# Weight tiles quantised inside the feed-forward loop, fewer in the first unit, and a reordered end of the main loop in a perceiver layer

## The chip, the cores and the metric

The kernel runs on one core of one Trainium2 chip. The metric is the device time of one execution in microseconds (us); the time shown for a kernel is the median of its runs. One further execution was taken with the hardware profiler, and all durations of single instructions come from it.

## The reference

Three blocks with residuals, on x of shape 8 x 64 x 512 (512 rows in all):

```python
x = x + cross_attention(layernorm(x), ctx)   # ctx 8 x 1601 x 256; 16 heads of 128; q and k rms-normalised
x = x + self_attention(layernorm(x))         # causal over 64 rows, 16 heads of 32
x = x + ffn(layernorm(x))

def ternary_quant(w):                        # groups of 64 along a row, in bf16
    scale = clip(mean(|w|), 1e-8)            # per group
    return clip(round(w / scale), -1, 1) * scale

def ffn(x):                                  # w_gate_up 4096 x 512, w_proj 512 x 2048
    gate, up = split(x @ ternary_quant(w_gate_up).T)
    return rms_norm(silu(gate) * up) @ ternary_quant(w_proj).T
```

## The kernel before

**Stages.** The work goes in this order, with the times of the profiled execution: query projections of the cross attention, two heads at a time in `two_heads(n)`, n = 0 to 8 (0 to 126 us); the main loop (126 to 1389); the last unit's softmax and value projections, "behind the loop" (1389 to 1470); output projection and self attention (1470 to 1612); the feed-forward gate and up products, r = 0 to 15, 128 hidden columns each (to 1666.5); the down projection (to the end).

**The main loop** has 16 units u (8 batches, 2 groups of 8 heads) of 6 steps q, 256 context rows each. `step(u, q)` (L1102) makes scores of unit u and, from u = 1 on, weighs the context with the probabilities of unit u - 1 in seven products of half size (`pair_products`, L893) and four for the tail of 65 rows (`tail_products`, L918). They add up in four PSUM accumulators y0 to y3. `gather_first` (L937) and `gather` (L949) combine these into the outputs `a`; the probabilities' row sums are spread over the partitions by TensorE (`spread_sum`, L980), inverted on VectorE (`invert_sums`, L985, four parts) and multiplied in (`divide_half`, L970; `finish`, L989). In the loop every engine's order is written out by hand. For the unit before the last these steps stand behind the loop, still by hand on TensorE and VectorE. After that only TensorE's order is by hand, and a scheduler places the other engines' instructions when the program is built.

**Quantising.** The weights of the feed-forward part are quantised in 48 units of 128 x 512, numbers 0 to 31 for `w_gate_up` and 32 to 47 for `w_proj`. One unit is: a load (`load_weights`, L333, 256 KB, SyncE's queue); Abs and Sign on ScalarE (`magnitudes`, L349); group sums `tot`, scale `scl`, threshold `thr`, mask `m`, mask times sign, and a difference `sg` on VectorE (`quantise`, L360); a second difference and a product (`signed`, L379); then `put_by` (L384): a 32 x 32 transpose on VectorE and four stores of 32 KB to the scratch tensor `fw` from SyncE's queue. The feed-forward part reads `fw` back in loads of eight units, 2 MB: `load_fgu` for the first 32 units, `load_fp(0)` for units 32 to 39 and `load_fp(1)` for 40 to 47, all issued from GpSimd's queue.

Six units are quantised in the head loop (n = 2 to 7, set by `N0 = 2`), six in unit 0 of the main loop (every step), three in unit 1, two in each of units 2 to 14 (steps 0 and 4), one in unit 15, and the last six behind the loop by

```python
while n_q < NQ:
    wf = load_weights(n_q, mB[last][:, 0, 0:1])
    signed(*quantise(n_q, *magnitudes(wf)))
    put_by(n_q)
    n_q += 1
```

where a one-column copy on GpSimd (L345) holds each load back until `mB` is there.

**The feed-forward loop** (L1746): for each r, 16 matmuls make gate and up in two PSUM tiles, of which each has two buffers; ScalarE computes Silu (`gt`, three buffers), VectorE the product `hr` (two buffers), ScalarE and VectorE split it in two parts `hT`, ScalarE squares it, and GpSimd adds the square to `acc` (L1764), whose sums give the rms factor behind the first 32 products of the down projection. Both `load_fp` are issued at r = 7. Square, output and other passing tiles share ten buffers with the tag `t2`.

Of the kernel before, what the change touches and what calls it, by code (L numbers as in the profile page):

```python
# [9 lines left out]
F32 = mybir.dt.float32  # L10
# [9 lines left out]
P = 128  # L20
# [8 lines left out]
def perceiver_kernel(  # L29
# [296 lines left out]
                    krP[a - b * TAIL : e - b * TAIL, b, ts(g, HG)], kr[a - n0 : e - n0, :]  # L326
                )

    N0 = 2
    quantised = {}  # L330
    wpool = [None]

    def load_weights(u, behind=None):  # L333

        if u < 2 * NF:
            src = w_gu[ts(u, P), :]
        else:
            hb, dt = divmod(u - 2 * NF, ND)
            src = w_fproj[ts(dt, P), ts(hb, 512)]
        if len(wpool) == 1:  # L340
            wf = block("wf", 0)
        else:
            wf = fq.tile([P, 512], F32, tag="wf", name="wf", bufs=1)
        if behind is not None:
            nc.gpsimd.tensor_copy(wf[:, 0:1], behind)  # L345
        nc.sync.dma_start(wf, src)
        return wf

    def magnitudes(wf):  # L349
        n = len(wpool)  # L350
        aw = wpool[0].tile([P, 8, 64], BF, tag="aw", name="aw", bufs=n)
        nc.scalar.activation(aw.rearrange("p g k -> p (g k)"), wf, AF.Abs)
        sg = wpool[0].tile([P, 8, 64], BF, tag="sg", name="sg", bufs=n)
        nc.scalar.activation(sg.rearrange("p g k -> p (g k)"), wf, AF.Sign)
        wT = aw
        if n == 1:
            wT = wpool[0].tile([P, 8, 64], BF, tag="wT", name="wT")
        return aw, sg, wT.rearrange("p g k -> p (g k)")

    def quantise(u, aw, sg, wT):  # L360

        tot = small.tile([P, 8], F32, tag="tot", name="tot")
        nc.vector.tensor_reduce(tot, aw, AX.X, ALU.add)
        scl = small.tile([P, 8], BF, tag="scl", name="scl")
        nc.vector.tensor_scalar(scl, tot, 1.0 / 64, SCALE_MIN, ALU.mult, ALU.max)

        thr = small.tile([P, 8], F32, tag="thr", name="thr")
        nc.vector.tensor_scalar(thr, scl, 257.0 / 512, None, ALU.mult)
        m = wpool[0].tile([P, 8, 64], BF, tag="m", name="m")
        nc.vector.tensor_tensor(  # L370
            m, aw, thr.unsqueeze(2).to_broadcast([P, 8, 64]), ALU.is_gt
        )
        nc.vector.tensor_tensor(m, m, sg, ALU.mult)
        nc.vector.tensor_tensor(
            sg, aw, scl.unsqueeze(2).to_broadcast([P, 8, 64]), ALU.subtract
        )
        return u, m, aw, sg, wT

    def signed(u, m, aw, nd, wT):  # L379
        nc.vector.tensor_tensor(nd, aw, nd, ALU.subtract)  # L380
        nc.vector.tensor_tensor(m, nd, m, ALU.mult)
        quantised[u] = m, wT

    def put_by(u):  # L384
# [13 lines left out]
    with tc.tile_pool(name="qphase", bufs=1) as qp, tc.tile_pool(  # L398
# [197 lines left out]
        with tc.manual_schedule(  # L596
# [70 lines left out]
                        xns_q.append(normalise(x_sb, i + 2, qp, mvs[i + 2], rstds[i]))  # L667
                    next(roots[i], None)
            head_sums(0)
            loaded, early = [], []  # L670
            for n in range(H // 2 + 1):
                if n + 1 < H // 2:
                    head_sums(n + 1)
# [216 lines left out]
        add_to_sums(u, NJF, nc.gpsimd)  # L890
        s_sb.pop((u, NJF))

    def pair_products(u, p):  # L893

        if p == 0:
            new_y(u, 4)
        b11, b21, b22, r1, r2, r3, n4 = yA.pop((u, p))
        for k, h, i, b_, first in (
            (0, 0, 0, b11, True),
            (1, 0, 1, b21, True),  # L900
            (2, 1, 2, n4, True),
            (0, 1, 3, r1, False),
            (1, 1, 4, r2, False),
            (2, 0, 6, b22, False),
            (3, 1, 5, r3, True),
        ):
            if i == 3:
                a = yB.pop((u, p))
            elif i < 3:
                (a11, a12), (_, a22) = prob_blocks(u, p)  # L910
                a = a11, a12, a22
            product(yps[u][k][:, ts(h, W // 2)], b_, a[i], first and p == 0)
            yield
        s_pair.pop((u, p))
        for i in range(2):
            s_sb.pop((u, 2 * p + i))

    def tail_products(u):  # L918
        s = s_sb[u, NJF][:TAIL].rearrange("p (j h) s -> p j (h s)", j=2)
        for c in range(NC):  # L920
            for j in range(2):
                k, h = ((1, 0), (2, 1), (2, 0), (3, 0))[2 * c + j]
                product(
                    yps[u][k][:, ts(h, W // 2)], cxn[u, NY - 1][:TAIL, 0, ts(c, P)], s[:, j], False
                )

    def halves_of(t):
        return [t[:, ts(h, W // 2)] for h in range(2)]
# [169 lines left out]
    def weigh(k):  # L1098
        for _ in range(k):
            next(under_way, None)  # L1100

    def step(u, q):  # L1102
# [9 lines left out]
        ssq = small.tile([P, 2, HG], F32, tag="ssq2", name="ssq2")  # L1112
        probs = PROBS[u == last].get(q, ()) if u > 0 else ()
        fw_tile = None
        tern = ((q in TERN and (u, q) != (last, 4)) or u == 1 and q == 2 or u == 0) and n_q < NQ
        if tern:
            wf = load_weights(n_q)

# [96 lines left out]
            fw_tile = magnitudes(wf)  # L1215


        product_7()
        squares(ssq[:, 1], 1, c22)
        s = work.tile([P, 2, HG, S], F32, tag="s", name="s", bufs=8)  # L1220
# [17 lines left out]
            spread_max(u - 1)  # L1238
        nc.scalar.copy(quarters[:, 2], s_a[:, 1])  # L1239
        squares(ssq[:, 0], 0, c11)  # L1240
        if u == last and q == NQU - 1:
            spread_sum(last - 1)
        if new:
            under_way = pair_products(*new)
            weigh(3)
        if halves:
            signed(*halves.pop())
            put_by(n_q - 1)
        if fw_tile:
            halves.append(quantise(n_q, *fw_tile))  # L1250
            n_q += 1
# [32 lines left out]
    with tc.manual_schedule(  # L1284
        engines={mybir.EngineType.PE, mybir.EngineType.DVE}
    ):

        while later:
            later.pop(0)()
        wv_sb.append(load_wv(1))  # L1290
        if halves:
            signed(*halves.pop())
            put_by(n_q - 1)
        weigh(9)
        prob_sums(last - 1, NQU - 1)
        tail_products(last - 1)
        s_sb.pop((last - 1, NJF))
        under_way = pair_products(last - 1, NQU - 1)
        weigh(3)
        find_max(last)  # L1300
        mB[last] = spread_diag(mB[last])
        for i in range(4):
            invert_sums(last - 1, i)
        weigh(2)
        gather_first(last - 1, nc.vector)
        weigh(1)
        g_last = gather(last - 1, nc.vector)
        next(g_last)
        divide_half(last - 1, 0)
        weigh(9)  # L1310
        load_contexts(NU * NY)
        for _ in g_last:
            pass
        divide_half(last - 1, 1)
    with tc.manual_schedule(engines={mybir.EngineType.PE}):
        for h in range(HG // 2):
            values(h, "ks")
        spread_max(last)
        for h in range(HG // 2, HG):
            values(h, "ks")  # L1320
        x_sb = wkv.tile([P, NTT, D], F32, tag="w", name="x_again")
        nc.gpsimd.dma_start(x_sb, xf.rearrange("(t p) d -> p t d", p=P))
        for j in range(NJ):
            less_max(last, (j,))
            exponentials(last, (j,))
            add_to_sums(last, j, nc.vector)
        n_wo = 0
        for j in range(NJ):
            weigh_context(last, j)
            if j == NJ - 3:  # L1330
                find_sum(last)
            if j == NJ - 2:
                spread_sum(last)
                for i in range(4):
                    invert_sums(last, i)
        while n_q < NQ:
            wf = load_weights(n_q, mB[last][:, 0, 0:1])
            signed(*quantise(n_q, *magnitudes(wf)))
            put_by(n_q)
            n_q += 1  # L1340
        for h in range(H):
            load_wo(h)
        wa_qk = big.tile([P, ND, 2 * D], F32, tag="A", name="wa_qk")
        nc.gpsimd.dma_start(
            wa_qk, w_attn[:, 0 : 2 * D].rearrange("(c p) n -> p c n", p=P)
        )
        wa_vp = big.tile([P, 2, ND, D], F32, tag="A", name="wa_vp")
        nc.gpsimd.dma_start(
            wa_vp[:, 0], w_attn[:, 2 * D :].rearrange("(c p) n -> p c n", p=P)
        )  # L1350
        nc.gpsimd.dma_start(wa_vp[:, 1], w_aproj.rearrange("(c p) n -> p c n", p=P))
        finish(last)


        x1 = x_sb
        ops = {0: ps.tile([P, D], F32, tag=turn_of("s"), name="op", bufs=1)}
        project(ops[0], 0, range(HG))
        for h in range(HG, H):
            values(h, "k")
# [15 lines left out]
    def blk(shape, name, dtype=F32):  # L1375
        return blkp.tile(shape, dtype, tag="blk", name=name)

    def t2(shape, name):
        return work.tile(shape, F32, tag="t2", name=name, bufs=T2)

    ba = small.tile([P, 2 * ND], F32, tag="ba", name="ba", bufs=1)
    nc.sync.dma_start(ba, b_attn[0 : 2 * D].rearrange("(j p) -> p j", p=P))
# [187 lines left out]
    with tc.manual_schedule(engines={mybir.EngineType.PE}):  # L1570
# [165 lines left out]
        def load_fp(k):  # L1736
# [5 lines left out]
            )  # L1742
            fp_sb.append(t)

        acc = aw_.tile([P, NT], F32, tag="oT", name="acc", bufs=1)
        for r in range(NF):  # L1746
            gu = [gus.get((r, i)) for i in range(2)]
# [11 lines left out]
            if r == 0:  # L1759
                nc.scalar.activation(acc, hr, AF.Square)  # L1760
            else:
                sq = t2([P, NT], "sq")
                nc.scalar.activation(sq, hr, AF.Square)
                nc.gpsimd.tensor_tensor(acc, acc, sq, ALU.add)  # L1764
            if r == NF // 2 - 1:
                for k in range(NF // 8):
                    load_fp(k)
        for t in range(NTT):
            op = ps.tile([P, D], F32, tag="m", name="fop", bufs=2)
            y = t2([P, D], "fy")  # L1770
# [80 lines left out]
```

## Time and profile before

| quantity | value |
|---|---|
| median of 3 runs | 1703.69 us (1703.57 to 1704.33) |
| profiled execution, its own time | 1703.88 us |
| its span, first to last instruction | 1702.0 us |
| mean granted TensorE clock | 0.995 |
| busy in the span: TensorE / VectorE / ScalarE / GpSimd | 1655.0 / 1289.8 / 1159.2 / 1032.1 us |
| TensorE busy from 1389 to 1470 us | 65.98 of 81 us, granted clock 0.92 |

In the profile PE is TensorE, PEld its weight loads, DVE VectorE, ACT ScalarE, POOL GpSimd, SP SyncE, whose queue only issues DMAs here. L numbers are lines of the kernel before. A line of the timeline gives start, duration, engine, line, operation, tiles and, in brackets, the idle time ahead of it with what ended it. A line of a table by windows gives the window, its length, and for each engine the busy time with the number of instructions, then the granted clock, the DMA share and GB/s.

### The profile page before, as it was taken

The numbers are of one execution on the slowest core, as the hardware profiler recorded it, in microseconds if no ns is written. First come the engines' busy times: TensorE is split into PE (matmuls) and PEld (weight loads), VectorE is DVE, ScalarE is ACT, GpSimd is POOL, SyncE is SP. The second block draws the span as 40 slices with busy tenths as digits, with TensorE's granted clock in tenths as the row PEclk, the third lists the DMA queues.
The fourth block names the chain that finished last, engine by engine and source line by source line (L and its number), as shares of the span: only waits on it lengthen the run. The fifth ranks groups of instructions, "written<-read, shape, count | busy, mean of one in ns | idle before, by whom it ended". The sixth has DMA issues, their size and how long they took to land.

```text
span 1702.0 us, 22178 instructions
## 1 busy us (share of the span) xinstructions
PE 1655.0 (97%) x6068; PEld 1060.6 (62%) x6068; DVE 1289.8 (76%) x1941; ACT 1159.2 (68%) x4511; POOL 1032.1 (61%) x1244
## 2 busy tenths in 40 slices
PE   9999899999999999999999999999999989899998
PEld 5655456666666666666666666666666553366787
DVE  5777988888888887888888888888788866545641
ACT  5768787878777777878787778777787743123441
POOL 3212257778787879787787878786978854100040
PEclk9999999999999999999999999999999999999999
DMA  7113221211212111211121221111212026600330
GB/s 228 13 15 64 46 53 43 44 42 38 45 40 44 35 42 43 47 43 35 44 45 41 43 41 38 44 36 47 49 29 55 22 82 230 148 1 1 100 99 25
DMA packets 254244, 92.74 MB, mean 54 GB/s; under 512 B 208400, under 2 KB 234792, under 8 KB 254120
## 3 DMA queue, kind: packets, MB, share of 16 engines
q1 hardware_dynamic: 244762, 68.78, 18.2%
q0 software_dynamic: 8928, 22.02, 4.3%
q8 instruction: 48, 0.79, 0.2%
q14 instruction: 76, 0.62, 0.1%
q10 hardware_dynamic: 430, 0.53, 0.1%
HBM read 77.62 MB, written 7.34 MB: 50 GB/s over the span
## 4 chain that ended last, share of the span: by engine, by line
PE 69%; DVE 12%; POOL 8%; ACT 5%; issue 3%; DMA 2%; SPq 0%; DVEq 0%; POOLq 0%; ACTq 0%
PE p_u L750 15%; PE y L750 12%; PE p L750 10%; PE s_a L750 10%; PE gu L1662 4%; PE op L1061 3%; PE fop L1780 2%; PE s L750 2%; PE mm_qk L1457 2%; DVE s L724 2%; ACT c L754 1%; DVE mx L740 1%; ACT p_u L754 1%; PE kp L302 1%; PE vp L1046 1%
## 5 line engine op out<-in xcount | busy, mean ns | idle before, releaser
L754 ACT ACTIVATE c<-c 128x128 f32<-128x128 f32 x1152 | 341.7, 302 | 104.7 <-DVE c L1185 68.6
L754 ACT ACTIVATION_READ_ACCUMULATOR c<-c 128x1 f32 x1152 | 220.7, 192 | 0.0
L750 PE MATMUL p_u<-wk,cxT 128*128 128x512 f32 x384 | 196.3, 593 | 1.1 <-ACT p_u L754 1.1
L724 DVE TENSOR_TENSOR s<-s,ssq 128x1024 f32<-128x1024 f32 x96 | 135.4, 1410 | 52.9 <-ACT ssq L105 52.9
L750 PE MATMUL y<-s,cxn 128*128 128x256 f32 x540 | 145.9, 379 | 0.0
L740 DVE TENSOR_TENSOR mx<-mx,s 128x512 f32<-128x512 f32 x160 | 134.3, 839 | 5.5
L750 PEld LDWEIGHTS s_a<-aT,cxS 128*128 128x128 f32 x384 | 72.8, 190 | 93.8 <-issue 78.0
L813 DVE TENSOR_TENSOR s<-s,mB 128x1024 f32<-128x1024 f32 (+1 forms) x102 | 126.7, 1255 | 2.1 <-ACT mB L791 2.1
L754 ACT ACTIVATE p_u<-p_u 128x128 f32<-128x128 f32 x384 | 100.4, 262 | 27.8 <-PE p_u L750 18.7
L878 POOL TENSOR_TENSOR yT<-s 128x256 f32<-128x256 f32 x76 | 73.7, 970 | 69.3 <-PE y L750 67.5
L750 PE MATMUL s_a<-aT,cxS 128*128 128x256 f32 x384 | 114.4, 380 | 1.3 <-ACT s L1239 1.3
L817 ACT ACTIVATE s<-s,zero_t 128x1024 f32<-128x1024 f32 (+1 forms) x102 | 112.0, 1099 | 4.8 <-DVE s L813 4.7
L750 PE MATMUL s_a<-aT,cxT 128*128 128x256 f32 x384 | 114.7, 380 | 0.5 <-ACT half L1171 0.5
L750 PEld LDWEIGHTS y<-s,cxn 128*128 128x128 f32 x540 | 102.7, 190 | 14.3
L750 PE MATMUL p_u<-wkS,cxT 128*128 128x512 f32 x192 | 102.4, 615 | 9.1 <-DVE c L1185 8.5
L750 PEld LDWEIGHTS s_a<-aT,cxT 128*128 128x128 f32 x384 | 73.1, 191 | 51.9 <-issue 41.2
L750 PE MATMUL p_u<-wkS,cxS 128*128 128x512 f32 x192 | 99.7, 601 | 2.4 <-POOL cxS L230 1.4
L1154 ACT COPY p<-p 128x512 f32<-128x512 f32 x96 | 56.1, 584 | 64.9 <-PE p L750 63.1
L750 PE MATMUL p<-wkS,cxS 128*128 128x512 f32 x192 | 98.8, 596 | 1.4 <-POOL cxS L228 1.4
L750 PE MATMUL p<-wk,cxS 128*128 128x512 f32 x192 | 98.3, 594 | 0.6 <-ACT p L1154 0.6
L750 PE MATMUL p<-wk,cxT 128*128 128x512 f32 x192 | 98.2, 593 | 0.5 <-DVE st L712 0.5
L1185 DVE TENSOR_TENSOR c<-p_u,p 128x512 f32<-128x512 f32 x96 | 63.7, 664 | 41.2 <-PE p_u L750 41.2
(276 smaller groups left out, 4321.3 us busy)
## 6 DMA issues: line engine op xcount, KB each, us to landing
cxn<-in_ctx_dram SPq DMA_DIRECT2D x96, 256.0 KB
cxB<-in_ctx_dram SPq DMA_DIRECT2D x192, 64.0 KB
wf<-in_L_ffn_w_gate_up_dram SPq DMA_DIRECT2D x32, 256.0 KB
fgu<-fw POOLq DMA_DIRECT2D x4, 2048.0 KB, 8.2
fw<-aw SPq DMA_DIRECT2D x168, 32.0 KB
wq<-in_L_xattn_Wq_dram SPq DMA_DIRECT2D x4, 1024.0 KB
wf<-in_L_ffn_w_proj_dram SPq DMA_DIRECT2D x16, 256.0 KB
wo<-in_L_xattn_Wo_dram POOLq DMA_DIRECT2D x16, 256.0 KB, 5.4
```

Of the source, the lines that this page charges most:

```text
L724: nc.vector.tensor_tensor(flat, flat, kr.unsqueeze(2).to_broadcast([P, 2 * HG, S]), ALU.mult)
L740: nc.vector.tensor_tensor(mx[u][:r], mx[u][:r], s[:r], ALU.max)
L750: nc.tensor.matmul(out_, a, w, start=start, stop=True, skip_group_check=not start)
L754: nc.scalar.activation(k[:, ts(h, HD)], k[:, ts(h, HD)], AF.Square, accum_out=ssq[:, 4 * half + h : 4 * half + h + 1],)
L813: nc.vector.tensor_tensor(t, t, m.to_broadcast([r, len(js), W]), ALU.subtract)
L817: nc.scalar.activation(t, t, AF.Exp, bias=zero_t[: t.shape[0]], scale=1.0)
L878: eng.tensor_tensor(s1, a21, a22, ALU.add)
L1061: nc.tensor.matmul(op, o_sb[h][:, ts(t, P)], wo_sb[h], start=(h == 0), stop=(h == H - 1),)
L1154: nc.scalar.copy(p5, p_5)
L1185: nc.vector.tensor_tensor(c22, p_u, p5, ALU.add)
L1457: nc.tensor.matmul(mm[:, j, :], wa_qk[:, c, ts(ND * i + j0 + j, P)], xT_a[:, c, cols], start=(c == 0), stop=(c == ND - 1),)
L1662: nc.tensor.matmul(gu[:, cols], fgu_sb[rr // 8][:, rr % 8, c, :], xs_[n_][c][:, cols], start=(c == 0 and n_ == 0), stop=(c == ND - 1 and n ...
```

## The change

Eight units (40 to 47, all of `load_fp(1)`) are quantised in the feed-forward loop, at r in `LATE`; the loop behind the main loop is gone. The head loop takes seven units (from n = 1), unit 0 three instead of six. In the feed-forward loop three of a unit's five elementwise operations on 128 x 512 go to GpSimd, the tiles come from the shared `t2` buffers, the load is held behind `gt` of its r by a one-column copy on GpSimd, and `load_fp(1)` is issued after the last unit. Separately, for the unit before the last, the row sums are spread ahead of `product_7` of the loop's last step and inverted in that step, the products run in an order that completes y0 and y1 first, and `gather_first`, the first part of `gather` and `divide_half(.., 0)` come ahead of `find_max` and of the remaining products.

```diff
-    N0 = 2
+    N0 = 1
...
-    def quantise(u, aw, sg, wT):
+    def quantise(u, aw, sg, wT, m=None, eng=nc.vector):
...
-        nc.vector.tensor_tensor(m, m, sg, ALU.mult)
+        eng.tensor_tensor(m, m, sg, ALU.mult)
...
-    def signed(u, m, aw, nd, wT):
-        nc.vector.tensor_tensor(nd, aw, nd, ALU.subtract)
-        nc.vector.tensor_tensor(m, nd, m, ALU.mult)
+    def signed(u, m, aw, nd, wT, eng=nc.vector):
+        eng.tensor_tensor(nd, aw, nd, ALU.subtract)
+        eng.tensor_tensor(m, nd, m, ALU.mult)
...
-            loaded, early = [], []
+            loaded, early = [load_weights(0)], []
...
-        tern = ((q in TERN and (u, q) != (last, 4)) or u == 1 and q == 2 or u == 0) and n_q < NQ
+        tern = ((q in TERN and (u, q) != (last, 4)) or u < 2 and q == 2) and n_q < NQ
...
+        if u == last and q == NQU - 1:
+            spread_sum(last - 1)
         product_7()
...
-        if u == last and q == NQU - 1:
-            spread_sum(last - 1)
...
             put_by(n_q - 1)
+        if u == last and q == NQU - 1:
+            for i in range(4):
+                invert_sums(last - 1, i)
...
         prob_sums(last - 1, NQU - 1)
-        tail_products(last - 1)
-        s_sb.pop((last - 1, NJF))
-        under_way = pair_products(last - 1, NQU - 1)
-        weigh(3)
-        find_max(last)
-        mB[last] = spread_diag(mB[last])
-        for i in range(4):
-            invert_sums(last - 1, i)
+        under_way = pair_products(last - 1, NQU - 1, (0, 1, 3, 4, 6, 2, 5))
+        weigh(2)
+        tail_products(last - 1, (0,))
         weigh(2)
         gather_first(last - 1, nc.vector)
+        tail_products(last - 1, (2,))
         weigh(1)
         g_last = gather(last - 1, nc.vector)
         next(g_last)
         divide_half(last - 1, 0)
+        find_max(last)
+        mB[last] = spread_diag(mB[last])
+        tail_products(last - 1, (1, 3))
+        s_sb.pop((last - 1, NJF))
         weigh(9)
...
-        while n_q < NQ:
-            wf = load_weights(n_q, mB[last][:, 0, 0:1])
-            signed(*quantise(n_q, *magnitudes(wf)))
-            put_by(n_q)
-            n_q += 1
...
+        LATE = (1, 3, 5, 7, 9, 11, 12, 13)
...
+            if r in LATE:
+                wf = t2([P, 512], "wf")
+                nc.gpsimd.tensor_copy(wf[:, 0:1], gt[:, 0:1])
+                load_weights(n_q, wf)
+                both = t2([P, 2, 8, 64], "aw", BF)
+                m = t2([P, 8, 64], "m", BF)
+                tern = quantise(
+                    n_q, *magnitudes(wf, (both[:, 0], both[:, 1])), m, nc.gpsimd
+                )
+                signed(*tern, nc.gpsimd)
+                put_by(n_q)
+                n_q += 1
             if r == NF // 2 - 1:
-                for k in range(NF // 8):
-                    load_fp(k)
+                load_fp(0)
+            if n_q == NQ and len(fp_sb) == 1:
+                load_fp(1)
```

More of the change, by code (lines that the diff above doesn't have):

```diff
@@ L327, in tail_roots, with load_weights @@
                 )
-    N0 = 2
+    N0 = 1
     quantised = {}
     wpool = [None]
-    def load_weights(u, behind=None):
+    def load_weights(u, wf=None):
         if u < 2 * NF:
@@ L339, in load_weights, with magnitudes @@
             src = w_fproj[ts(dt, P), ts(hb, 512)]
-        if len(wpool) == 1:
+        if wf is None and len(wpool) == 1:
             wf = block("wf", 0)
-        else:
+        elif wf is None:
             wf = fq.tile([P, 512], F32, tag="wf", name="wf", bufs=1)
-        if behind is not None:
-            nc.gpsimd.tensor_copy(wf[:, 0:1], behind)
         nc.sync.dma_start(wf, src)
         return wf
-    def magnitudes(wf):
+    def magnitudes(wf, rooms=None):
         n = len(wpool)
-        aw = wpool[0].tile([P, 8, 64], BF, tag="aw", name="aw", bufs=n)
+        aw, sg = rooms or [
+            wpool[0].tile([P, 8, 64], BF, tag=n_, name=n_, bufs=n) for n_ in ("aw", "sg")
+        ]
         nc.scalar.activation(aw.rearrange("p g k -> p (g k)"), wf, AF.Abs)
-        sg = wpool[0].tile([P, 8, 64], BF, tag="sg", name="sg", bufs=n)
         nc.scalar.activation(sg.rearrange("p g k -> p (g k)"), wf, AF.Sign)
@@ L368, in quantise @@
         nc.vector.tensor_scalar(thr, scl, 257.0 / 512, None, ALU.mult)
-        m = wpool[0].tile([P, 8, 64], BF, tag="m", name="m")
+        if m is None:
+            m = wpool[0].tile([P, 8, 64], BF, tag="m", name="m")
         nc.vector.tensor_tensor(
@@ L891, in last_sums, with pair_products @@
         s_sb.pop((u, NJF))
-    def pair_products(u, p):
+    def pair_products(u, p, order=(0, 1, 2, 3, 4, 6, 5)):
         if p == 0:
@@ L897, in pair_products @@
         b11, b21, b22, r1, r2, r3, n4 = yA.pop((u, p))
[L898 to L909, printed above, removed]
+        places = (
+            (0, 0, b11, True),
+            (1, 0, b21, True),
+            (2, 1, n4, True),
+            (0, 1, r1, False),
+            (1, 1, r2, False),
+            (3, 1, r3, True),
+            (2, 0, b22, False),
+        )
+        for i in order:
+            k, h, b_, first = places[i]
+            if i >= 3:
+                a = yB[u, p][i]
+            else:
                 (a11, a12), (_, a22) = prob_blocks(u, p)
-                a = a11, a12, a22
-            product(yps[u][k][:, ts(h, W // 2)], b_, a[i], first and p == 0)
+                a = (a11, a12, a22)[i]
+            product(yps[u][k][:, ts(h, W // 2)], b_, a, first and p == 0)
             yield
+        yB.pop((u, p))
         s_pair.pop((u, p))
@@ L916, in pair_products, with tail_products @@
             s_sb.pop((u, 2 * p + i))
-    def tail_products(u):
+    def tail_products(u, which=(0, 1, 2, 3)):
         s = s_sb[u, NJF][:TAIL].rearrange("p (j h) s -> p j (h s)", j=2)
[L920 to L925, printed above, removed]
+        for i in which:
+            c, j = divmod(i, 2)
+            k, h = ((1, 0), (2, 1), (2, 0), (3, 0))[i]
+            product(
+                yps[u][k][:, ts(h, W // 2)], cxn[u, NY - 1][:TAIL, 0, ts(c, P)], s[:, j], False
+            )
     def halves_of(t):
@@ L1376, in blk, with t2 @@
         return blkp.tile(shape, dtype, tag="blk", name=name)
-    def t2(shape, name):
-        return work.tile(shape, F32, tag="t2", name=name, bufs=T2)
+    def t2(shape, name, dtype=F32):
+        return work.tile(shape, dtype, tag="t2", name=name, bufs=T2)
     ba = small.tile([P, 2 * ND], F32, tag="ba", name="ba", bufs=1)
@@ L1743, in load_fp @@
             fp_sb.append(t)
+        LATE = (1, 3, 5, 7, 9, 11, 12, 13)
+        assert n_q + len(LATE) == NQ and n_q >= 2 * NF + 8
         acc = aw_.tile([P, NT], F32, tag="oT", name="acc", bufs=1)
@@ L1764, in perceiver_kernel @@
                 nc.gpsimd.tensor_tensor(acc, acc, sq, ALU.add)
+            if r in LATE:
[6 more added lines that the diff above has]
+                    n_q, *magnitudes(wf, (both[:, 0], both[:, 1])), m, nc.gpsimd
+                )
+                signed(*tern, nc.gpsimd)
+                put_by(n_q)
+                n_q += 1
             if r == NF // 2 - 1:
-                for k in range(NF // 8):
-                    load_fp(k)
+                load_fp(0)
+            if n_q == NQ and len(fp_sb) == 1:
+                load_fp(1)
         for t in range(NTT):
```

## Prediction

> **What bounds the kernel now.** I read the page's totals first: TensorE is busy for 97% of the span, so only its idle stretches and what follows them can be won.
>
> ```profile
> PE 1655.0 (97%) x6068; PEld 1060.6 (62%) x6068; DVE 1289.8 (76%) x1941; ACT 1159.2 (68%) x4511; POOL 1032.1 (61%) x1244
> ...
> PEclk9999999999999999999999999999999999999999
> ```
>
> Second, TensorE's timeline behind the main loop, where the brackets are its idle time.
>
> ```profile
> 1396.59 9.54 PE L1046 MATMUL vp<-a,wv 128*128 128x512 f32 x16 [5.45 <-issue]
> 1406.20 7.03 PE L1046 MATMUL vp<-a,wv 128*128 128x512 f32 x16
> ...
> 1424.82 10.54 PE L841 MATMUL y<-s,cxn 128*128 128x512 f32 x24 [1.29 <-DMA cxn<-in_ctx_dram]
> ...
> 1451.88 6.04 PE L1046 MATMUL vp<-a,wv 128*128 128x512 f32 x8 [7.47 <-DVE a L993]
> ```
>
> Two holes, 5.45 and 7.47 us. The 16 matmuls behind the first take 9.54 us, the next 16 take 7.03: in the table by windows the granted clock is 0.50 from 1397 to 1400 and again from 1452 to 1456, so each hole costs some 2.5 us more. Third, what filled the holes:
>
> ```profile
> 1391.05 3.38 DVE L987 RECIPROCAL rB<-rB 128x128 f32<-128x128 f32 x4
> ...
> 1445.64 0.63 ACT L352 ACTIVATE aw<-wf 128x512 bf16<-128x512 f32 x1 [10.88 <-DMA fw<-aw]
> 1446.18 0.57 ACT L983 COPY rB<-bp 128x512 f32<-128x512 f32 x1
> ```
>
> In the first hole VectorE inverts the sums, then gathers; in the second the copy that the inversion needs stands on ScalarE behind a quantising step that waited 10.88 us for stores. Fourth, unit 0 by step (columns: PE, PEld, DVE, ACT, POOL busy):
>
> ```profile
> 163.00:176.30 13.30, 13.12 (x40) 7.12 (x39) 11.30 (x20) 10.62 (x47) 2.92 (x5) 1.00 0.30 50
> 176.30:189.20 12.90, 10.89 (x32) 5.31 (x31) 11.84 (x22) 10.28 (x48) 1.88 (x5) 1.00 0.31 54
> 189.20:201.50 12.30, 10.96 (x33) 5.67 (x32) 11.44 (x20) 8.32 (x38) 3.20 (x4) 1.00 0.22 38
> 201.50:213.00 11.50, 9.02 (x28) 4.30 (x28) 10.94 (x18) 9.49 (x46) 2.41 (x5) 1.00 0.20 37
> 213.00:226.00 13.00, 11.71 (x39) 6.64 (x38) 11.71 (x22) 11.16 (x53) 4.87 (x8) 1.00 0.37 64
> ```
>
> VectorE is dense and TensorE idle for 0.18 + 2.01 + 1.34 + 2.48 + 1.29 = 7.3 us. Last, the feed-forward part and the rows that price what moves there:
>
> ```profile
> 1666.53 7.56 PE L1780 MATMUL fop<-fp,hT 128*128 128x512 f32 x32
> ...
> L1764 POOL TENSOR_TENSOR acc<-acc,sq x15: 1287/1296/1732, 1619.7 to 1668.8; 128x512 f32<-128x512 f32 x15
> L881 POOL TENSOR_TENSOR s<-s x90: 721/728/1182, 223.6 to 1384.6; 128x256 f32<-128x256 f32 x90
> L381 DVE TENSOR_TENSOR m<-sg,m x48: 424/560/837, 56.8 to 1470.4; 128x512 bf16<-128x512 bf16 x48
> DMA to landing us min/median/max: 8.5/10.1/11.7
> ```
>
> TensorE has no gap there, 3.68 us per r (16 x 0.23). The last row is `load_fp`.
>
> **Gains, part by part.** *End of the loop.* The inversion moves into VectorE's wait of 3.19 us ahead of L724 in the last step, so it costs 0.2 us there. Behind the loop POOL's last pair sum still ends at 1388.15; maxima (to 1388.9), gather and half a division (2.4 us) then let the first `vp` start near 1391.5, when TensorE has just finished the remaining products. The hole of 5.45 shrinks by 5.1 and its half clock goes (9.54 - 6.98 = 2.6), less 1.2 us, since the copy of the first `vp` out of PSUM now queues behind the second half of the gather on VectorE: -6.4. *Behind it.* Without quantising, spread sums at 1435.8 give copy 0.6, inversion 3.4, `finish` 1.3: ready by 1441.3, while `op` matmuls cover TensorE until 1444.4. The hole of 7.47 goes, with its slow clock (6.04 - 3.49 = 2.6) and two gaps of 0.29 and 0.38: -10.7. The 1.29 us wait for `cxn` I leave: its load shares the queues with the weights whose loads GpSimd no longer holds back (0 to +3). *Unit 0.* A unit costs VectorE 4.4 us (0.67 + 0.19 + 0.17 + 0.69 + 0.42 + 0.69 in one step, 0.41 + 0.42 + 0.71 in the next). Two fewer in the dense stretch take 8.7 of its 46 busy us; ScalarE is next with 50 of 63 from 163 to 226. Of 7.3 us I take 5.5 (3 to 7.3). *Head.* n = 1 now has a unit: from 10.37 us (spacing of L534) to the 11.85 of n = 2, +1.5; and its load leaves SyncE's queue behind eleven small stores at 36.7, lands 3.05 later (as issue 1408.03 to Abs 1411.08 shows), while ScalarE reaches Abs at 37.3: +2.4 in front of the copies that TensorE needs. Head +3.9 (1.5 to 5). Sum: -6.4 - 10.7 - 5.5 + 3.9 = -18.7 (-24 to -11).
>
> **The price in the feed-forward loop.** The order in which the changed program's instructions stand on each queue decides. On VectorE the transpose of unit k stands ahead of the group sums of unit k + 1, and waits for POOL's last product of unit k; behind it wait the next `lo` and `hr`, hence the PSUM tiles and TensorE. So units do not overlap: one round runs VectorE, POOL, VectorE. On SyncE the load of k + 2 stands behind the four stores of k; on ScalarE Abs, waiting for that load, stands ahead of a Silu. On POOL a round holds product, `acc`, difference, product. The three bf16 operations on POOL are in no trace. By elements they are `acc`, 1.30 us; by bytes L881, 0.73. I take 1.30, since rows of POOL follow the element count (0.73 for 256, 1.30 for 512), and nothing shows that a narrower type is faster there.
>
> One round: `tot`, `scl`, `thr`, `m` 0.67 + 0.19 + 0.17 + 0.69, POOL 4 x 1.30 (the 0.69 of `sg` lies under `acc`), transpose 0.71, one `hr` 0.69, hand-offs 0.5: 8.8 us. TensorE makes two r in 7.4, and r = 11, 12, 13 have a unit each, so the backlog only grows. Start: Silu of r = 1 ends at 1617.5, copy 0.4, load 3.05, Abs 0.6, hand-offs: 1622.0. Eight rounds end at 1692.4; going through the queues item by item, the second and third rounds take 11 us (loads that wait for SyncE, two `acc`), which makes the last transpose end at 1697.9. Four stores of 0.62, the last landing 1.6 after its issue: 1702.0. `load_fp(1)`, alone, 8.5: **1710.6**. TensorE's loop also stretches by 10 us, but ends at 1676, does the half that `load_fp(0)` feeds, and then waits for some 30 us. Before, it read the first tile of `load_fp(1)` at 1666.53 + 3.68 = 1670.2. So the end moves by 40.4, plus 2.6 for the half clock after so long a hole: +43.0. With 0.73 per operation the load lands at 1697.9 (+30.3); with 1.7, if VectorE's work in between slows POOL as L826 (1.27, at most 2.25) was slowed, at 1719.8 (+52.2).
>
> Here a rule speaks against the change. VectorE needs 0.42 us for these bf16 products at their best, so POOL's 1.30 would be three times that. The Trainium skill, GPSIMD Engine Reference, section 8, calls VectorE structurally about twice as fast for elementwise work. By that ratio an operation would be an estimated 0.84 us, the load would land near 1700 and the sum be some 10 us lower. No run shown here decides between them.
>
> Sum: -18.7 + 43.0 = +24.3, span 1726.3; the profiled execution lies 1.9 above its span and 0.2 above the median: **1728**.
>
> **Rivals.** *Slow POOL.* At 2.0 us per operation `load_fp(1)` lands at 1726.7: +40, 1744. For it: VectorE is busy between POOL's steps. Against: `acc`, beside the same VectorE work, shows 1.30. *The front gains fail.* A late `cxn` or POOL's pair sums keep the first hole: 8 us back, 1736. *Faster: no backlog.* If units overlap and only the last one's own chain counts, Silu of r = 13 at 1658.2 gives copy and load 3.6, Abs 0.6, VectorE 1.8, POOL 3.9, `sg` and transpose 1.4, stores 4.1, load 8.5, hand-offs 0.6: 1682.7, so +12.5 + 2.6 - 18.7 = -3.6, 1700; with 0.73 on POOL 1698. It wins once the last transpose ends before 1673.5. Against: only two loads are ahead at any time, and the order on VectorE. *Nothing moves:* excluded, as all 48 units and their queues are in the built program.
>
> **How the numbers follow.** Main case 0.62, 1712 (0.73 us per POOL operation and the largest front gains) to 1740 (1.7 us and the middle ones); slow POOL 0.16; failed front gains 0.10; no backlog 0.12, of which 0.10 falls under -0.2% (3.4 us, about what the runs can tell from no change). Range 1706 to 1746: it leaves out the case without backlog and the upper part of slow POOL.
>
> **What would show it.** Right: idle PE behind the first 16 `fop` matmuls, ended by the load `fp`, 20 to 45 us long, then a clock near 0.5; `fw` stores at the end of the trace after 1675; the holes ahead of `vp` gone; POOL's bf16 rows near 1.3. Wrong: `load_fp(1)` landing less than 16 us after TensorE reaches it, or gaps left behind the main loop.

## The result, and the profile after

The changed kernel takes 1728.45 us (median of 4 runs, 1728.17 to 1729.88), the kernel before 1703.63 us beside it: a ratio of 1.0148, 95% interval 1.013 to 1.0165, or 25 us longer. Its profiled execution, the longest of the four, took 1729.88 us with a span of 1728.1 us, 26.1 us more than before.

From here on, L numbers are lines of the kernel whose trace is shown. First the totals of the page of after and the clock in forty slices (43 us each):

```profile
PE 1656.6 (96%) x6068; PEld 1063.6 (62%) x6068; DVE 1287.4 (74%) x1917; ACT 1160.2 (67%) x4511; POOL 1055.3 (61%) x1270
...
PEclk9999999999999999999999999999999999999978
```

TensorE's work is the same; the idle time lies in the last two slices. Its timeline in after, first at the end of the main loop (the two holes ahead of `vp` were there), then in the down projection:

```profile
1391.33 7.05 PE L1049 MATMUL vp<-a,wv 128*128 128x512 f32 x16
...
1437.01 13.90 PE L1049 MATMUL vp<-a,wv 128*128 128x512 f32 x32
...
1660.68 4.12 PE L1796 MATMUL fop<-fp,hT 128*128 128x512 f32 x16
1694.69 5.82 PE L1796 MATMUL fop<-fp,hT 128*128 128x512 f32 x16 [29.89 <-DMA fp<-fw]
```

Both holes are gone and the `vp` matmuls run at 7.05 us for 16. The price is above all one hole of 29.89 us, ended by the load `fp`; the 16 matmuls behind it take 5.82 us, the first 3.3 us of them at a granted clock of 0.50. GpSimd's and VectorE's own timelines show what the load waited for: the last transpose, four stores, then the issue:

```profile
1680.57 0.71 DVE L387 STREAM_TRANSPOSE aw<-m 128x512 bf16<-128x512 bf16 x1 [2.49 <-POOL m L381]
...
1686.41 0.93 POOL L1740 DMA_DIRECT2D fp<-fw  x1 [5.88 <-DMA fw<-aw]
```

The eight transposes start at 1612.9, 1623.5, 1634.8, 1645.0, 1655.5, 1664.3, 1672.5 and 1680.6: rounds (from one transpose to the next) of 8.1 to 11.3 us, one after the other.

Where the time went, by the same instruction in both traces (before to after):

| place | shift against before |
|---|---|
| first copy `p1` of the main loop (127.06 to 133.59) | +6.5 |
| unit 1, same matmul (295.39 to 296.01) | +0.6 |
| unit 14 (1295.84 to 1296.22) | +0.4 |
| last step (1369.77 to 1368.67) | -1.1 |
| first `vp` behind the loop (1396.59 to 1391.33) | -5.3 |
| r = 3 of the feed-forward loop (1618.68 to 1600.25) | -18.4 |
| end of the span | +26.1 |

So in these two traces the head cost 6.5 us, unit 0 gave back 5.9, and the front as a whole gained 18.4; the feed-forward part cost 44.5. Of these, 12.6 are TensorE's loop, stretched by the rounds (the first `fop` comes at 1660.68 instead of 1666.53, although the front gained 18.4), 29.9 are the hole, and the remaining 2.0 are the slow clock behind it.

### The profile page after: what moved, and what is told of

It reads as the page before. It is cut to its first block, busy times and chain, and to the rows that moved or that the text cites. A ratio compares the mean times of both kernels' runs of the same rounds, so it can differ in the third digit from the quotient of the medians.

```text
span 1728.1 us, 22175 instructions
## 1 busy us (share of the span) xinstructions
PE 1656.6 (96%) x6068; PEld 1063.6 (62%) x6068; DVE 1287.4 (74%) x1917; ACT 1160.2 (67%) x4511; POOL 1055.3 (61%) x1270
## 4 chain that ended last, share of the span: by engine, by line
PE 68%; DVE 12%; POOL 9%; ACT 4%; issue 3%; DMA 2%; SPq 0%; DVEq 0%; POOLq 0%; ACTq 0%
PE p_u L750 15%; PE y L750 12%; PE p L750 10%; PE s_a L750 10%; PE op L1064 3%; PE kp L302 2%; PE s L750 2%; PE mm_qk L1458 2%; PE fop L1796 2%; PE vp L1049 2%; DVE s L724 2%; ACT c L754 1%; DVE mx L740 1%; ACT p_u L754 1%; POOL den L883 1%
```

## The experiments

Chips differ by one or two us, so each run is judged by its ratio to the kernel before, timed beside it; 0.001 is 1.7 us. Against the kernel as changed (1.0148), differences of ratios are used; by the intervals of the two ratios, such a difference is uncertain by some 4 us.

**The front alone.** LATE is empty, and `load_fp(1)` reads units 32 to 39.

```diff
-        LATE = (1, 3, 5, 7, 9, 11, 12, 13)
+        LATE = ()
...
-            u = 2 * NF + 8 * k
+            u = 2 * NF
```

> The changed kernel with units 40 to 47 left out: they are not quantised at all, and the second load of the down projection reads units 32 to 39 again (so its output means nothing). Theory A (the whole price is the late second load, the front part gains what its trace shows, TensorE 18.5 us earlier at the first gate and up products): 1685 us. Rival B (part of the price lies elsewhere, for example in the shared buffers or in load and store traffic that the front part moved): over 1690 us. Rival C (the front part gains less than 10 us by itself): 1694 us or more.

Measured: 1683.54 us, ratio 0.9888 (0.9873 to 0.9904): -19.1 us against before. The front is worth what the trace says, and the units in the feed-forward part cost 0.026 or 44.3 us. Theory A holds; B and C fall.

**The reordered end alone**, with head, unit 0 and six units behind the loop as before.

> The kernel before with the reordered end of the main loop alone (sums spread and inverted in the last step, half the accumulators gathered first); the head, unit 0 and the six units behind the loop as before. Theory A (the prediction's step): the first hole goes with its half clock, -6.4 us, 1697 us. Rival B (GpSimd's last pair sum or the copies hold the first values back): -2 us or less, 1702 us. Rival C (what is gained is given back at the second hole, since the six units behind the loop end when they ended): 1702 to 1704 us, with the second hole wider than 7.5 us.

Measured: 1697.40 us, ratio 0.9966 (0.9953 to 0.9978): -5.8 us. TensorE's timeline of this run:

```profile
1391.14 7.05 PE L1049 MATMUL vp<-a,wv 128*128 128x512 f32 x16
...
1443.68 5.89 PE L1049 MATMUL vp<-a,wv 128*128 128x512 f32 x8 [7.19 <-DVE a L996]
```

The first hole is gone; the second is as long as it was (7.19 us), only earlier. Theory A.

**The load of unit 0 early in the head.**

```diff
             load_wq(3)
+            loaded, early = [load_weights(0)], []
...
-            loaded, early = [load_weights(0)], []
```

> The changed kernel with the load of unit 0 issued ahead of the small stores in the head (before the query projections, behind the last weight load) instead of after them. Theory A (in the head, ScalarE's wait of 2.77 us for this load opened a hole of 3.93 us on TensorE, and the half clock behind it cost about as much as the prediction's other term): the hole and the slow clock go, 4 to 5 us: 1723.5 us. Rival (the prediction's own figure of 2.4 us is all there is to it): 1726 us. Rival (the load takes bandwidth from the first weights, which TensorE waits for): 1728 us or more.

Measured: 1725.08 us, ratio 1.0135 (1.0122 to 1.0149): 2.2 us earlier than the changed kernel, between the figures of theory A and the first rival, and the intervals overlap. The traces say more. TensorE in after, ScalarE in after, then the copy `p1` in before, after and this run:

```profile
41.19 2.05 PE L490 MATMUL q_u<-xS,wqS 128*128 128x256 f32 x4 [3.93 <-ACT qp L532]
```

```profile
39.63 0.63 ACT L352 ACTIVATE aw<-wf 128x512 bf16<-128x512 f32 x1 [2.77 <-DMA wf<-in_L_ffn_w_gate_up_dram]
```

```profile
127.06 0.59 ACT L1129 COPY p<-p_u 128x512 f32<-128x512 f32 x1 [2.91 <-PE p_u L750]
```

```profile
133.59 0.59 ACT L1132 COPY p<-p_u 128x512 f32<-128x512 f32 x1 [2.91 <-PE p_u L750]
```

```profile
129.15 0.59 ACT L1132 COPY p<-p_u 128x512 f32<-128x512 f32 x1 [2.91 <-PE p_u L750]
```

The hole shrinks to 1.06 us, and the granted clock is 1.00 from 41 to 45 us where after had 0.50; the head costs 2.1 us instead of 6.5. So 4.4 us of the head were the late load with its half clock in these two profiled executions. But after is the extreme: nine other runs of this document have the same head, and in their traces the hole is 1.67 to 3.63 us and `p1` comes at 129.44 to 133.36, 2.4 to 6.3 us later than before, 5.0 in the median. What the late load costs thus differs from trace to trace, which fits the 2.2 us that show over all runs.

**GpSimd's operations on VectorE.** `m, nc.gpsimd` becomes `m` and `signed(*tern, nc.gpsimd)` becomes `signed(*tern)`.

> The changed kernel with the three operations of the late units on VectorE instead of GpSimd. Theory A (the rounds go from VectorE to GpSimd and back, each waiting for the other): a unit keeps VectorE 4.4 us and the round has no hand-off and no acc in it; with hr and the low part of two r VectorE needs 7.2 us per two r, where TensorE needs 7.4. Only r = 11 to 13 with a unit each fall behind: last transpose near 1657, load landed near 1670, TensorE waits 10 to 20 us: 1705 us (1698 to 1712). Rival (loads and stores through SyncE's queue set the rounds of 8 to 11 us): 1722 us or more.

Measured: 1720.77 us, ratio 1.0098 (1.0082 to 1.0113): 8.5 us earlier, 9 us above the range of theory A and at the rival's edge. Two things were wrong in the expectation. VectorE was nearly never idle in a round and still needed 8 us, as some of its operations were stretched (a difference to 1.67 us, a low part `hT` to 1.79). And the scheduler put eight stores in a row ahead of two loads. SyncE's queue in this run, and ScalarE's wait for the load:

```profile
1618.25 10.56 SPq L390 DMA_DIRECT2D fw<-aw  x8
1628.98 2.07 SPq L344 DMA_DIRECT2D wf<-in_L_ffn_w_proj_dram  x2
```

```profile
1633.33 0.63 ACT L352 ACTIVATE aw<-wf 128x512 bf16<-128x512 f32 x1 [3.42 <-DMA wf<-in_L_ffn_w_proj_dram]
```

One round took 15.9 us by it. GpSimd's hand-offs are not the only link.

**Loads from GpSimd's queue.** `load_weights` issues the late loads with `nc.gpsimd.dma_start`.

> The changed kernel with the loads of the eight late units issued from GpSimd's queue, right behind the one-column copy, so that none stands behind the four stores of a unit before it on SyncE's queue. Theory A (each round goes from VectorE to GpSimd and back, and the load behind the stores is a part of it): ScalarE's Abs waited 2.30, 1.78, 2.09, 1.58, 1.35 and 2.21 us for a load in the trace of after, 11.3 us in all; GpSimd pays up to 0.9 us for each issue: 4 to 11 us earlier, 1717 to 1724 us. Rival (the loads lie beside GpSimd's part of the round and cost nothing): 1728 us or more, since only GpSimd's issues are added.

Measured: 1729.71 us, ratio 1.0162 (1.0148 to 1.0176): 2.4 us later, which the intervals do not tell from no change. The rival's number, but not its reason: Abs still waited (3.91, 0.91, 3.73, 0.83, 3.94 and 0.79 us, 14.1 in all where after had 11.3), since the loads now stand behind a difference of the unit before or a sum `acc` on GpSimd's queue. The load was moved from one queue to another and not out of the round, so this run decides nothing about the load's share.

**Parts of the round taken out.** Next the load was left out (one tile for all units), GpSimd's work halved, and both at once.

```diff
-                wf = t2([P, 512], "wf")
+                if r == LATE[0]:
+                    wf = t2([P, 512], "wf")
+                    load_weights(n_q, wf)
                 nc.gpsimd.tensor_copy(wf[:, 0:1], gt[:, 0:1])
-                load_weights(n_q, wf)
```

```diff
-        eng.tensor_tensor(m, m, sg, ALU.mult)
+        eng.tensor_tensor(m[:, :4], m[:, :4], sg[:, :4], ALU.mult)
```

> The changed kernel in which all eight late units use the one tile that the first of them loaded (the other seven loads are left out; the one-column copy that holds a unit back stays). Theory A (the load is one more link of the ring): ScalarE's waits for it, 11.3 us in all, go: 1716 us. Rival (the load runs beside GpSimd's products and the store's issue; without it Abs would wait for the buffers instead): 1724 us or more.

> The changed kernel with GpSimd's three operations of a late unit cut to half of their columns (four of eight groups; the other half is left out). Theory A (a round is a ring VectorE, GpSimd, VectorE, in which GpSimd's time counts in full): the rows go from 1.15 to an estimated 0.6 us, 1.6 us less in each of eight rounds: 13 us earlier than the changed kernel, 1714 us. Rival (the rounds wait for loads that stand behind stores on SyncE's queue, or for VectorE's own queue, and what GpSimd saves becomes waiting): 4 us earlier at most, 1723 us or more.

> Both of the two cuts at once: GpSimd's three operations on half of their columns, and one loaded tile for all eight late units (half of the products and seven loads are left out). Each alone gave 8.5 and 3.9 us. Theory A (links of one ring): the two add, 12.4 us earlier than the changed kernel, 1715 us. Theory B (GpSimd's products and the next load are two branches of a round side by side, and each hides a part of the other): more than the sum, since neither hides the other any more: 17 us or more, 1710 us or less. Theory C (VectorE's own queue is the floor: 1.7 us of sums and mask, 0.7 to 1.8 for the difference, 0.7 for the transpose and 2.8 for hr and the low parts of two r, 6 to 7 us, beside 7.4 of TensorE for two r): no round under 7 us, so little more than one of the two alone, 1718 us.

| left out | ratio (95%) | against the changed kernel | last transpose starts |
|---|---|---|---|
| seven loads | 1.0125 (1.0110 to 1.0141) | -3.9 us | 1674.4 |
| half of GpSimd's columns | 1.0098 (1.0083 to 1.0113) | -8.5 us | 1668.9 |
| both | 1.0064 (1.0050 to 1.0077) | -14.3 us | 1664.5 |

Without the loads Abs waits for none (its longest wait is 0.62 us), and yet 3.9 of the expected 11 us show: the number is the rival's, its reason is not. One round grew to 13.9 us instead. GpSimd's and VectorE's operations stand in another order there, and a low part `hT` on VectorE, ahead of the transpose, took 4.26 us beside three operations of GpSimd in a row:

```profile
1625.48 4.26 DVE L140 TENSOR_TENSOR hT<-hr,hT 128x512 fp32r<-128x512 f32 x1 [0.69 <-ACT hT L139]
```

Halving GpSimd's columns took its operations to 0.67 to 1.06 us, 11.1 us less over the 24 of them, and gave 8.5; Abs still waited 12.3 us for loads. Together the two gave 14.3 us where the sum is 12.4. This agrees with theory A (a ring to which GpSimd and the load each add). Theory C does not fit, as three rounds took 6.6 us, under its floor of 7; B's 17 us are not excluded by the intervals. Even then the rounds were 6.6 to 11.8 us and TensorE waited 19.6 us for the load: that much of the price is left with VectorE's links, the other half of GpSimd's columns, and the stores and the load at the end; how it divides was not tried.

**The second load in halves.**

```diff
+            if n_q == NQ - 4 and len(fp_sb) == 1:
+                load_fp_half(0)
+            if r == LATE[-1]:
+                load_fp_half(1)
```

> The changed kernel with the second load of the down projection issued as two halves of 1 MB: units 40 to 43 as soon as they are stored, 44 to 47 at the end. Theory A (TensorE's 29.9 us wait is ended by the last load alone, 8.2 us from its issue for 2 MB): a half lands some 4 us sooner and the 16 matmuls of each quarter go ahead: 1724 us. Rival (the landing is set by the stores or the queue, not by the size): 1728 us.

Measured: 1722.65 us, ratio 1.0123 (1.0109 to 1.0137): 4.3 us earlier, the number of theory A. Issue to TensorE's start took 5.5 us (1684.65 to 1690.18) where the whole load took 8.3 (1686.41 to 1694.69). So 2.8 us are the smaller load; the other 1.7 by which TensorE started earlier are an earlier issue, as the last transpose came 1.5 us sooner in this trace.

**Other places for the eight units.** First in the main loop, then behind it.

```diff
+ or 2 <= u < 10 and q == 3
```

> The changed kernel with units 40 to 47 quantised in the main loop, in step q = 3 of units u = 2 to 9, instead of the feed-forward loop. Theory A: nothing is late in the feed-forward part, and what is paid is VectorE's time in the loop. VectorE is busy 10.15 of 12.2 us in such a step and 8.55 of 12.3 in the next; a unit adds 2.8 and 1.5 us, so it overruns the first step by 0.8 us: 8 x 0.8 = 6.4 us, 1691 us (1685 with no cost, 1700 if each unit costs as much as one of the three in unit 0 that went, 5.9 / 3 = 2 us). Rival (the feed-forward part stays long for another reason): over 1720 us.

Measured: 1704.27 us, ratio 1.0011 (1.0002 to 1.0020), 20.9 us more than without the units, 2.6 each and not 0.8. TensorE's timeline in step 4 of such a unit, which now has two units' work:

```profile
423.94 1.12 PE L750 MATMUL p_u<-wk,cxT 128*128 128x512 f32 x2 [1.73 <-ACT p_u L754]
```

The wait is for ScalarE's squares of `p_u`, an engine that the expectation had not counted. It shows in every second of the eight units; the other four have a wait of 1.14 us for the same squares and one of 0.92 for VectorE. Together these are 15 of the 20.9 us, 11.5 of them for ScalarE; what makes up the rest stays open.

```diff
+        while n_q < NQ:
+            wf = fq.tile([P, 512], F32, tag="wf", name="wf", bufs=1)
+            nc.gpsimd.tensor_copy(wf[:, 0:1], held[:, 0:1])  # held: inverted sums of the last unit
...
     xs.close()
```

> The changed kernel with the eight late units quantised again behind the main loop, on VectorE, but each load held until the last sums are inverted and the units written behind the last value projections, not ahead of the copy that the inversion needs; nothing in the feed-forward loop. From 1430 to 1490 us VectorE is busy 10.8 of 60 us and ScalarE 4.6 there. Theory A (the second hole of before came from where the units stood, not from their work; nothing else is late): 1683.5 us of the kernel without these units plus 0 to 6 us for copies that now stand behind a unit: 1686 us. Rival (the units cost TensorE what they cost before, 10.7 us and more, since there are eight of them instead of six): 1698 us.

Measured: 1702.65 us, ratio 1.0001 (0.9993 to 1.0010). The expectation was wrong by 16 us; the rival's 1698 was nearer. TensorE and VectorE in this run:

```profile
1492.02 1.97 PE L1445 MATMUL tp_ln<-ident,xn 128*128 128x128 f32 x8 [13.39 <-DVE xn L131]
```

```profile
1470.27 0.69 DVE L362 TENSOR_REDUCE tot<-aw 128x8 f32<-128x512 bf16 x1 [8.85 <-ACT aw L352]
```

The four units done by 1459 us cost one hole of 1.88; the other four waited for their loads (Abs 7.53 us in one case), and the next stage's normalised rows `xn` stood behind them on VectorE.

**Four and four.** This points to a mixture: four units behind the loop, four at r = 0 to 3, and the load of unit 0 early.

```diff
+        while n_q < NQ - 4:
...
+        LATE = (0, 1, 2, 3)
```

> Four late units (40 to 43) behind the loop as in the run with all eight there, where the first four were done by 1459 us at the price of one hole of 1.9 us, and four (44 to 47) in the feed-forward loop at r = 0 to 3; the load of unit 0 early. Theory A (what costs is the number of rounds in a row after r = 1: four of some 10 us end near 1643, stores by 1648, the load lands near 1656, and TensorE, stretched by some 5 us, gets there at about the same time): 1683.5 of the kernel without the units, -3 for the head, +2 behind the loop, +5 in the feed-forward loop: 1688 us (1684 to 1696). Rival (the hole ahead of the second half of the down projection stays, since the rounds are paced by r and the load by its own 8 us): over 1700 us.

Measured: 1692.22 us, ratio 0.9934 (0.9921 to 0.9946): faster than both kernels, 11 us under the kernel before. TensorE's three longest waits behind the loop in this run:

```profile
1437.51 10.72 PE L1049 MATMUL vp<-a,wv 128*128 128x512 f32 x24 [2.26 <-DVE o_h L1060]
...
1617.01 0.50 PE L1671 MATMUL gu<-xT_f,fgu 128*128 128x512 f32 x1 [2.78 <-DVE hr L1768]
1624.27 0.50 PE L1671 MATMUL gu<-xT_f,fgu 128*128 128x512 f32 x1 [1.73 <-DVE hr L1768]
```

The hole in the down projection is gone. With the transposes at 1605.6, 1613.4, 1621.2 and 1633.7 the load is issued at 1639.7, and 8.5 us later it is there before TensorE needs it. Theory A, 4 us above its figure and inside its range. The early load of unit 0 is part of this gain; alone it gave the changed kernel 2.2 us.

## Why the prediction was right, step by step

The forecast was 1728 us in 1706 to 1746; measured 1728.45. The mechanism and the order of the steps were right: one late load behind rounds that do not overlap. That the median agrees to half a us is luck: terms were off by up to 2.6 us, the head (+2.6), the price (+1.5) and the clock near 1340 (-1.5) above all; they left 1.8 us in the span (26.1 against 24.3), and the profiled execution is 1.4 us longer than the median.

- **Sum of the front: -18.7; measured -18.4 in the trace, -19.1 by the run without the late units.** *End of the loop*, -6.4: -5.8 alone. *Behind it*, -10.7: from the first `vp` (-5.3) to r = 3 (-18.4) lie 13.1 us, of which 2.5 are the slow clock of the first 16 (9.54 to 7.05) that the prediction counted with the end: 10.6. The wait for `cxn` stayed, 1.81 instead of 1.29.
- **Unit 0: -5.5; measured -5.9.**
- **Head: +3.9; measured +6.5 in this trace, 5.0 in the median of nine others. This term was mis-sized**: its range was 1.5 to 5. ScalarE's wait was right (2.77 for 2.4), but in front of TensorE it became 3.93 us, and no half clock was put behind it, though the prediction had one behind each of the other holes: 0.50 from 41 to 45 us. The Trainium skill, TensorE: Matmul & The Clock Gate, Part 1, names idle gaps over some 3.4 us, judged in a free-running window, as what halves the clock. The 3.93 us here agree; but shorter holes of this case halved it too (last section), and there the measurement decides.
- **Not foreseen: -1.5 us near 1340,** where nothing was changed. Both traces have the same hole there, and only before lost its clock; this is chance, not a gain of the change:

```profile
1339.99 2.04 PE L750 MATMUL p_u<-wkS,cxT 128*128 128x512 f32 x2 [2.06 <-DVE c L1185]
```

```profile
1340.40 1.12 PE L750 MATMUL p_u<-wkS,cxT 128*128 128x512 f32 x2 [2.07 <-DVE c L1188]
```

- **Price in the feed-forward loop: +43.0; measured 44.5 in the trace and 44.3 by the runs.** TensorE started on the late load at 1694.69, in the time scale of before 1713.1, against 1710.6 predicted for the landing. TensorE waited 29.9 us ("some 30"), and its loop stretched by 12.6 instead of 10. The 3.05 us put down for a load were read from an Abs that came straight behind a copy, where they are only an upper bound; in after the six loads that Abs waited for took 2.97 to 5.87 us from their issue to Abs.
- **The rounds**, 8.8 us with two of 11: measured 8.1 to 11.3, four of them above 10; the mean from the first transpose to the last is (1680.57 - 1612.94) / 7 = 9.7. Two `acc` stand in each of these four, where the prediction had them in two rounds only. (Its two rounds of 11 us move the last transpose from 1692.4 to 1696.8; the other 1.1 us up to its 1697.9 are in no sum that it shows.) GpSimd's operations were 1.15 us undisturbed instead of 1.30; six of the 24 took 1.48 to 1.54, so that the mean, 1.25, came near the forecast partly by luck. VectorE's difference, put at 0.69 and "under `acc`", took 1.75 in six of eight units. GpSimd's two products (L373, L381) and VectorE's difference (L374) in after, with duration min/median/max in ns, first and last start; of L374 the first row is the main loop and head, the second the late units:

```profile
L373 POOL TENSOR_TENSOR m<-m,aw x8: 1149/1160/1488, 1606.0 to 1675.2; 128x512 bf16<-128x512 bf16 x8
L381 POOL TENSOR_TENSOR m<-aw,m x8: 1148/1154/1168, 1611.8 to 1679.4; 128x512 bf16<-128x512 bf16 x8
```

```profile
L374 DVE TENSOR_TENSOR sg<-aw,scl x40: 691/693/1110, 43.7 to 1316.0; 128x512 bf16<-128x512 bf16 x40
L374 DVE TENSOR_TENSOR aw<-aw,scl x8: 689/1752/1765, 1607.5 to 1676.3; 128x512 bf16<-128x512 bf16 x8
```

- **The rule weighed in the prediction** (VectorE about twice as fast) would have given 0.84 us per operation; the rows show 1.15 against 0.42, a factor of 2.7. The element count was the better guide: 1.15 lies nearer to 1.30 than to 0.73, and half the columns, 128x256 in bf16, took 0.67 us, near the 0.73 of 128x256 in f32.
- **Rivals.** Slow POOL: none of the 24 bf16 operations took over 1.6 us, where the rival had 2.0. Front gains fail: both holes are gone. No backlog: the transposes follow one another without overlap, and only with four units (the mixture) does the end come in time. What a cheaper GpSimd operation is worth was put about right: from 1.30 to 0.73 us the prediction's sum fell by 12.7 us, which is some 10 us for the 0.46 us per operation by which the run with halved columns was cheaper; it gave 8.5, within its uncertainty.

## What to carry to other kernels

Work that is moved into another loop to fill an engine's idle time is paid by the length of its chain, not by its busy time: count the hand-offs on every in-order queue, the DMA queue's too, and multiply by the units in a row before the consumer. A few such units may be free where eight are not: four and four in two places, with the load of unit 0 early, gave 0.9934, eight in any one place 1.000 to 1.015. And every hole of more than 3 us that a forecast adds on TensorE is given its half clock as well; for one of 1.8 to 3 us it came in about half of the cases in these traces.

## What was not expected of the hardware

VectorE's difference and GpSimd's sum `acc` exclude each other, as the timelines of after show side by side, first VectorE, then GpSimd:

```profile
1607.50 1.76 DVE L374 TENSOR_TENSOR aw<-aw,scl 128x512 bf16<-128x512 bf16 x1 [1.07 <-POOL m L373]
```

```profile
1607.42 1.28 POOL L1767 TENSOR_TENSOR acc<-acc,sq 128x512 f32<-128x512 f32 x1
```

The difference begins 0.08 us behind `acc` and ends 0.56 behind its end, as it would if it waited for `acc` and then took most of its own 0.69. It does so in six of the eight late units (1.73 to 1.76 us); in the other two, at 1631.56 and 1668.92, GpSimd is idle and it takes 0.69. The 4.26 us of `hT` in the run without loads are the same: it ended 0.60 us behind the third of GpSimd's operations. The Trainium skill, SBUF — State Buffer, section "SBUF: two separate sides", says that a VectorE operation with two SBUF inputs and a GpSimd operation that reads SBUF take a port pair in turn, each for a whole instruction; these numbers agree. `hr`, whose first input is in PSUM, kept its time beside `acc` (0.68 at 1609.18).

A hole of 2.06 us halved TensorE's clock in one trace and one of 2.07 did not in the other (granted clock 0.50 and 1.00 in the 2.4 us from 1341). All fourteen traces of this case have this hole, at 2.06 or 2.07 us; six lost their clock behind it and eight did not. Over all of TensorE's holes of 1.4 us and more behind its first matmuls in these traces, none up to 1.81 us was followed by a slow clock, 18 of 38 between 1.82 and 3.03 us were, and every one of 3.25 us or more was; once, in the run with GpSimd's operations on VectorE, a hole of 1.20 us was too. What decides in between no run here shows; a hole of about 2 us is thus priced between nothing and 1.7 us of slow clock: from 1339.99 and from 1340.40 the same matmuls up to `y` take 3.52 and 1.83 us.
